# A list schedule that groups runs of quarter products and counts each change of tiling on TensorE

## The chip, the core and the metric

The kernel runs on one core of a Trainium2 chip. The metric is the device time of one execution in microseconds (us). TensorE is called PE here, VectorE DVE, ScalarE ACT, GpSimd POOL and the engine that issues the transfers SP, as in the profile.

## What is computed

Four layers follow each other on x of 128 graphs x 64 nodes x 256 features, all in fp32, with one 64 x 64 matrix adj for all graphs. Each layer is x = x + f(relu(layernorm(x))).

```python
# layer 0: two graph convolutions, then LSTMs over windows of p = 1..4 nodes
h = relu(adj @ (h @ Wg0 + bg0));  h = relu(adj @ (h @ Wg1 + bg1))
for p in 1, 2, 3, 4:
    wins = h[:, :nw * p].reshape(B * nw, p, D)          # nw = 64 // p
    h[:, p - 1 :: p] = lstm_last(Wih[p - 1], Whh[p - 1], bias, wins)
# layer 1: x' = L_norm @ x, a norm, attention of 4 heads masked by adj, an MLP, norms
# layer 2: attention from two vectors, softmax over adj, then (attention @ h) @ W
# layer 3: U^T h, two dense layers, then U (...): U the eigenvectors of a Laplacian of adj
```

L_norm needs the largest eigenvalue of adj, layer 3 all eigenvectors; the kernel works them out itself.

## The kernel before

Two graphs (128 tokens) make a tile. Eight tiles make one of eight groups of layer 0 (plan groups 0 to 7); layers 1 to 3 run on half-groups of four tiles (sixteen of them, plan groups REST = 10 to 25). `WEIGHTS` (8) and `ATTN` (9) are the loads and preparations of the later layers' weights, which take the place of the LSTM weights in SBUF; `EIG` (1000) is the eigenvector work, a long chain of small VectorE operations.

Nothing is issued in the order in which it is written. Each call is recorded as an `Op` of a `Plan`, with an engine, an assumed cost, and what it depends on. `Plan.schedule` then makes one order for each engine: a list schedule on an assumed clock `now[e]` of each engine. Among the operations that are ready on an engine it takes the one with the smallest rank, and `issue` writes the instructions in that order. The chip's engines run their own queues in that order, and wait on semaphores where the real times differ from the plan's. Two things limit what may be taken: `window`, how many groups ahead of the oldest unfinished one an operation may be, and the buffers (`big`, `mid`, `stat`, and eight PSUM `bank`s), of which some are kept in reserve for the oldest group.

The rank of an operation is its group (clamped), then the longest path of plan costs behind it; `EIG` goes first on PE and last elsewhere.

A *quarter product* is a product of 64 x 64 by 64 x 64 in one quarter of the PE array: multiplying by a block-diagonal matrix of two graphs (`mix`), or attention of one head (`layer1`). They are recorded in a `burst`: 32 of them (16 in the first group and in the second convolution of layer 3) are one operation of the plan, so they stay together in PE's queue. There are 132 bursts: 36 in layer 0 and 96 in layers 1 to 3 (six for each half-group). All other work on PE uses the full array of 128 rows. The plan charges a burst 0.1 + 0.034 us a product and knows nothing of what stands beside it.

Layer 0 (`layer0`) has a front (norms, two graph convolutions with their bursts, the products with Wg) and then the LSTM steps: for each of two halves of the hidden size the gates' products, sigmoid and tanh on ACT, and three VectorE operations. Every instruction is recorded through one helper, so all have one source line (L332) in the profile, and work is told apart by tiles: `adjTb` is the matrix of the convolutions of layer 0, `lapb`, `Ub` and `UTb` those of layers 1 and 3, `bank` any PSUM bank, `mids` the gates.

## Time and profile before

| | |
|---|---|
| time, median of 3 runs | 2208.51 us (2205.82 to 2208.59) |
| span of the profiled run | 2203.4 us, granted PE clock 0.998 |
| instructions | 42,023, of them 15,428 matmul records |
| quarter products on PE | 7,680 records of 64 x 64, each product two |
| DMA | 36.46 MB, 4.5% of the engines' time on the main queue |

Where the prediction speaks of the profile: the page gives busy time by engine and the chain of work that ended last; a table of stretches gives busy time of each engine between two times; the list of waits says for which engine and tile PE waited; and the timeline gives starts, merged over equal neighbours. Full fp32 products are two records as well, transposes one. Layer 0 fills the time up to about 1,390 us, with the first instruction of layer 1 on PE at about 1,247 us.

### The profile page before, as it was taken

What the parts mean: (1) busy time and instruction counts of PE and PEld (TensorE: products, weight loads), DVE (VectorE), ACT (ScalarE), POOL (GpSimd) and SP (SyncE); (2) the same over time, 40 slices, a digit from 0 to 9 for tenths busy, and PEclk for the clock granted to TensorE, in tenths of its full rate; (3) what the DMA queues carried; (4) which work ended last, traced back from release to release, by engine and by line L of the source; (5) the groups of instructions that cost most, each with busy time, mean ns of one, the idle gap of its engine ahead of it and who ended that gap; (6) DMA issues with size and microseconds to landing.
All of it is one profiled execution on the core that took longest, in us unless ns stands there. A gap on an engine that the chain in (4) does not pass through costs nothing.

```text
span 2203.4 us, 42023 instructions
## 1 busy us (share of the span) xinstructions
PE 2176.4 (99%) x15428; PEld 1494.9 (68%) x15428; DVE 1689.4 (77%) x7018; ACT 967.3 (44%) x1943; POOL 554.3 (25%) x856
## 2 busy tenths in 40 slices
PE   9999999999999999999999999999999999999998
PEld 6578468468558558558557657777767677776776
DVE  7678767769999999999885525468797678776697
ACT  4332443433323433423423533355466555455674
POOL 3101110200100100100100304145374546444353
PEclk9999999999999999999999999999999999999999
DMA  7000000010000000000000011000000000000001
GB/s 258 2 3 22 2 2 20 2 39 1 1 1 1 1 1 1 1 1 1 6 0 1 6 41 33 1 1 12 11 11 11 30 11 30 19 13 1 1 2 59
DMA packets 32255, 36.46 MB, mean 17 GB/s; under 512 B 8113, under 2 KB 29489, under 8 KB 31537
## 3 DMA queue, kind: packets, MB, share of 16 engines
q1 hardware_dynamic: 30944, 32.73, 4.5%
q8 instruction: 121, 1.98, 0.4%
q10 hardware_dynamic: 1104, 1.05, 0.2%
q14 instruction: 86, 0.70, 0.1%
HBM read 22.85 MB, written 10.49 MB: 15 GB/s over the span
## 4 chain that ended last, share of the span: by engine, by line
PE 86%; DVE 9%; POOL 2%; ACT 1%; issue 1%; DMA 0%; SPq 0%; DVEq 0%; ACTq 0%; POOLq 0%
PE bank L332 86%; DVE arena L332 3%; DVE stat L332 2%; DVE big L332 2%; DVE x L332 1%; POOL stat L332 1%; DVE mids L332 1%; ACT mids L332 0%; DVE Whh L332 0%; ACT arena L332 0%; ACT big L332 0%; POOL big L332 0%; POOL x L332 0%; ACT x L332 0%; DMA adj<-in_adj_dram 0%
## 5 line engine op out<-in xcount | busy, mean ns | idle before, releaser
L332 PE MATMUL bank<-big,Wih 128*128 128x512 f32 (+2 forms) x2312 | 772.5, 477 | 1.0 <-POOL big L332 0.5
L332 ACT ACTIVATE mids<-bank,bl 128x256 f32<-128x256 f32 (+2 forms) x624 | 343.5, 562 | 600.2 <-PE bank L332 587.0
L332 PEld LDWEIGHTS bank<-big,Wih 128*128 128x128 f32 x2312 | 430.4, 190 | 248.9 <-issue 153.1
L332 PE MATMUL bank<-big,Whh 128*128 128x256 f32 (+2 forms) x1608 | 495.1, 443 | 2.1 <-DVE big L332 2.1
L332 PEld LDWEIGHTS bank<-big,Whh 128*128 128x128 f32 x1608 | 302.7, 190 | 132.0 <-issue 60.3
L332 DVE TENSOR_TENSOR arena<-arena 64x21 f32<-64x21 f32 (+5 forms) x2255 | 360.1, 191 | 33.0 <-POOL arena L332 1.0
L332 POOL TENSOR_SCALAR stat<-stat 128x4 f32<-128x4 f32 (+1 forms) x228 | 62.2, 274 | 689.8 <-DVE stat L332 676.7
L332 DVE TENSOR_TENSOR big<-big,mids 128x256 f32<-128x256 f32 (+2 forms) x192 | 98.2, 511 | 138.3 <-ACT mids L332 136.9
L332 DVE TENSOR_TENSOR big<-mids 128x512 f32<-128x512 f32 (+2 forms) x246 | 136.4, 559 | 59.4 <-ACT mids L332 56.5
L332 PE MATMUL bank<-arena,Wih 128*128 128x512 f32 (+2 forms) x408 | 146.0, 500 | 0.9 <-DVE Wih L332 0.4
L332 ACT ACTIVATE mids<-big 128x256 f32<-128x256 f32 (+2 forms) x176 | 89.8, 510 | 103.8 <-DVE big L332 75.2
L332 DVE SCALAR_TENSOR_TENSOR arena<-arena 64x1 f32<-64x1 f32 (+15 forms) x567 | 116.2, 229 | 12.7 <-POOL arena L332 6.2
L332 POOL TENSOR_TENSOR stat<-stat,mhalf 128x4 f32<-128x4 f32 (+1 forms) x114 | 119.3, 1049 | 5.7
L332 PEld LDWEIGHTS bank<-arena,Wih 128*128 128x128 f32 x408 | 76.3, 190 | 51.4 <-issue 33.7
L332 DVE TENSOR_SCALAR arena<-arena 64x1 f32<-64x1 f32 (+9 forms) x537 | 102.1, 198 | 9.2 <-POOL arena L332 1.0
L332 ACT COPY mids<-bank 128x256 f32<-128x256 f32 (+1 forms) x132 | 57.0, 488 | 78.0 <-PE bank L332 73.7
L332 DVE BATCH_NORM_STATS2 stat<-x 128x6 f32<-128x256 f32 x232 | 84.8, 409 | 0.1
L332 POOL MEMSET arena<- 64x2 f32 (+5 forms) x72 | 7.9, 112 | 295.1 <-DVE arena L332 295.1
L332 POOL TENSOR_TENSOR arena<-arena 64x1 f32<-64x1 f32 x66 | 39.2, 594 | 166.0 <-DVE arena L332 102.2
L332 POOL TENSOR_TENSOR big<-big,B1T 128x512 f32<-128x512 f32 x28 | 30.9, 1111 | 187.0 <-DVE stat L332 169.7
L332 PE MATMUL bank<-Wih,big 128*128 128x256 f32 (+1 forms) x320 | 73.5, 366 | 0.9 <-DVE big L332 0.8
L332 PE MATMUL bank<-Wg,mids 128*128 128x256 f32 x256 | 64.6, 393 | 0.7 <-ACT mids L332 0.7
(351 smaller groups left out, 3361.5 us busy)
## 6 DMA issues: line engine op xcount, KB each, us to landing
x<-in_x_dram SPq DMA_DIRECT2D x7, 1024.0 KB, 14.1
out_dram<-x SPq DMA_DIRECT2D x24, 256.0 KB, 2.3
Wih<-in_WihT_dram SPq DMA_DIRECT2D x3, 1024.0 KB, 16.0
Whh<-in_WhhT_dram SPq DMA_DIRECT2D x3, 1024.0 KB, 12.0
put<-x SPq DMA_DIRECT2D x2, 1024.0 KB, 4.0
arena<-put SPq DMA_DIRECT2D x2, 1024.0 KB, 5.1
out_dram<-arena SPq DMA_DIRECT2D x8, 256.0 KB, 2.2
Whh<-in_W_dram SPq DMA_DIRECT2D x2, 512.0 KB, 3.9
```

The costliest lines, as they stand in the source:

```text
L332: getattr(self.engines[op.eng], name)(*map(real, args), **{k: real(a) for k, a in kw.items()})
```

## The change

The order of work changes, and nothing else: no instruction is added or removed. Three things do it.

- The plan now remembers whether PE last ran quarter products (`many`). Each change between these and full products costs 0.178 us on its clock, and a burst itself 0.029 us a product.
- A new term `back`, ahead of the group's rank, puts an operation of PE back. In a run of quarter products, full products stand back behind any burst that is ready. Outside one, a burst stands back unless two are ready or it has been ready for 20 us (layers 1 to 3; in layer 0 it doesn't stand back).
- The front of layer 0 has `lead` = 1: it ranks with the group in front of it, by its path, so it goes ahead of that group's LSTM. For layer 0 the path alone decides within a group, as it did.

```diff
         yield
-        self.run.cost = 0.1 + 0.034 * len(self.run.calls)
+        self.run.cost = 0.029 * len(self.run.calls)
         self.run.lat = self.run.cost + 0.22
+        self.run.many = True
...
+                runs = sum(op.many and op.ready <= now[e] for op in ops)
...
-                    rank = (t > now[e] + 1e-9, t if t > now[e] + 1e-9 else 0.0, self.rank(op))
+                    back = many and not op.many and e == "PE" or op.many and not many and runs < 2 and now[e] - op.ready < (0.0 if op.group < REST else 20.0)
+                    rank = (t > now[e] + 1e-9, t if t > now[e] + 1e-9 else 0.0, back, self.rank(op))
...
+            if e == "PE" and op.many != many:
+                many, cost, lat = op.many, cost + 0.178, lat + 0.178
...
-        g = min(max(op.group, 0), self.ends)
+        g = min(max(op.group - op.lead, 0), self.ends)
+        if op.group < REST:
+            return (g, 0, -op.path, op.index)
         return (g, 6 * max(op.group - g, 0) - op.path, op.index)
...
     def layer0(x):
+        plan.lead = 1
...
                 G.tensor_tensor(dst, dst, b1[1], op=ALU.add)
+        plan.lead = 0
         cs, hs = fm(), fm()
```

## The prediction

> **What bounds the kernel now.** First the page: share of each engine, then the chain that ended last.

> ```profile
> PE 2176.4 (99%) x15428; PEld 1494.9 (68%) x15428; DVE 1689.4 (77%) x7018; ACT 967.3 (44%) x1943; POOL 554.3 (25%) x856
> PE 86%; DVE 9%; POOL 2%; ACT 1%; issue 1%; DMA 0%; SPq 0%; DVEq 0%; ACTq 0%; POOLq 0%
> ```

> PE is busy 99% and carries 86% of the chain. A busy PE is not proof by itself, because the ends of matmuls are modelled[...]. So I go by starts. Next the busy time by stretch (us and instructions of PE, PEld, DVE, ACT, POOL, then clock, DMA share, GB/s): the start, layer 0, the change-over, layers 1 to 3, the tail.

> ```profile
> 0.00:100.00 100.00, 95.94 (x687) 59.61 (x688) 69.83 (x399) 37.10 (x90) 26.91 (x74) 0.97 0.42 143
> 100.00:1290.00 1190.00, 1187.22 (x5831) 781.93 (x5831) 965.61 (x4860) 440.68 (x985) 103.57 (x217) 1.00 0.02 6
> 1290.00:1390.00 100.00, 97.01 (x360) 67.77 (x359) 41.84 (x65) 34.17 (x69) 27.86 (x23) 1.00 0.13 37
> 1390.00:2150.00 760.00, 753.10 (x7776) 550.04 (x7774) 573.26 (x1580) 434.29 (x760) 375.20 (x513) 1.00 0.03 11
> 2150.00:2204.00 54.00, 43.10 (x779) 35.52 (x778) 38.88 (x118) 21.08 (x42) 20.77 (x29) 0.98 0.18 60
> ```

> PE idles 4.1, 2.8, 3.0, 6.9 and 10.9 us: 27.7 in all. No other engine is near its limit outside layer 0, where the eigenvectors' work fills the VectorE. So there are two things to win or lose: the PE's own work, and these idle stretches. What ends them, from the waits of PE for 100 to 1340 us (first two rows) and for 1340 to 2150 us (the rest); columns: total us, times, longest.

> ```profile
> PE bank L332 <- DVE mids L332: 1.4, 4, 0.4
> PE bank L332 <- POOL big L332: 0.5, 1, 0.5
> ...
> PE bank L332 <- DVE big L332: 2.1, 1, 2.1
> PE bank L332 <- ACT arena L332: 1.7, 3, 0.8
> PE bank L332 <- ACT x L332: 1.2, 1, 1.2
> ```

> Many small waits with different releasers, none systematic.

> **What a run of quarter products costs.** The timeline of PE (start, duration, count) shows one run of 64 records (one burst of 32 products; each product is two records[...]) and one of 128 (two bursts together):

> ```profile
> 1233.16 3.62 PE L332 MATMUL bank<-Wg,mids 128*128 128x256 f32 x16
> 1236.71 1.16 PE L332 MATMUL bank<-adjTb,mids 64*64 64x64 f32 x64
> 1237.80 0.70 PE L332 MATMUL bank<-Wg,mids 128*128 128x256 f32 x2
> ...
> 389.66 3.17 PE L332 MATMUL bank<-big,Wg 128*128 128x512 f32 x7
> 392.75 2.10 PE L332 MATMUL bank<-adjTb,mids 64*64 64x64 f32 x128
> 394.78 0.49 PE L332 MATMUL bank<-arena 128*128 128x128 f32 x2
> ```

> Full matmuls of 256 columns start 0.2157 us apart, of 512 columns 0.4293 us (medians of starts in the trace). 16 x 0.2157 = 3.45, so a next full matmul could have started at 1236.61; the run starts at 1236.71 and the next full matmul at 1237.80. The run took 1.19 us of PE, 0.10 of it before its first start. For 128 records: 389.66 + 7 x 0.4293 = 392.67, next 394.78, so 2.11 us. Two runs apart cost 2.38, together 2.11. Over all runs the medians are 1.185 us (64 records, 82 runs) and 2.119 us (128 records, 9 runs); a run of 192 took 3.052. That is a line: 0.0146 us a record, plus **0.25 us a run** (2 x 1.185 - 2.119 = 0.251).

> [...] going in costs 0.094 us beyond the full matmul's usual 0.216, coming out the rest.

> **The change part by part.**

> 1. *Adjacent runs (rank term `back`, `runs`, and 0.178 a change in the plan's clock).* Counting the changed program's PE instructions: 3,840 quarter products in both, but they stand in 83 runs instead of 113. Layer 0 goes from 31 to 30, layers 1 to 3 from 82 to 53; there single bursts fall from 71 to 21, pairs rise from 8 to 23, threes from 3 to 8, and one run has five. Saved: 30 x 0.251 = **7.5 us**. All but one of these merges lie before the last 100 us of PE work, where PE is busy over 99%, so each comes off the end unless a wait swallows it. If every wait after 1390 us (6.9 us) swallowed what it could of the savings, about 4 would be left: the low bound of this part; the high one is 7.5.

> 2. *The burst's price in the plan (0.029 a product instead of 0.1 + 0.034).* For 32 products 0.93 us plus two changes at 0.178 makes 1.28 for a lone run, against 1.19 measured (before: 1.19). No instruction changes; it acts through the order alone, so its time is in the other parts.

> 3. *Layer 0 up to the second graph convolution ranks with the group in front (`lead`).* Bursts and normalisations of group g+1 go before the LSTM of group g. It adds no instruction. It should remove the waits in which a burst came too soon after the operation that feeds it: four waits on "DVE mids", 1.4 us. In the new order I compared, for each PE instruction, the PE work standing between it and the PE instruction its operands come from with the durations of the ACT, VectorE and GpSimd operations in between (0.5 to 0.8 us each with the hand-over, an estimate from the rows of the page). Before, 7 places in layer 0 after the first 100 us don't fit; after, 4. In layers 1 to 3 up to the tail 6 become 2; in the tail 22 become 21. I book **-1.5 us** and keep -5 and +5 as ends.

> 4. *What it makes worse.* A lone burst of layers 1 to 3 is held up to 20 us until a second is ready. PE takes other ready work meanwhile, so it costs nothing while eight half-groups are in flight; what is queued behind the burst is only its own half-group's chain. And at the change-over three bursts (half-groups 10, 11, 12) now stand together in front of the last LSTM steps of group 7, where one stood before. The copies that empty the banks of two of them stand on ACT some 90 us of PE work later, because the SBUF tiles they write come free only when group 7 is done. Four of eight banks are held meanwhile, a fifth for the first half of it by a weight preparation, so the LSTM turns over on three and then four banks. A gate of 336 columns is 4 products x 2 x 0.282 = 2.26 us of PE, and its sigmoid on ACT 0.5, so three banks suffice in the steady state; at the step's edge fewer input products can be moved forward (about 3 x 1.1 = 3.4 us of them) to hide the sigmoid, the three VectorE operations, the tanh and the product (six operations, some 2.8 us when VectorE runs at 0.45 us each). That still hides it. It doesn't while GpSimd runs its fourteen additions to x (1.3 us each, some 20 us), when VectorE operations took 1.0 to 1.9 us in the trace: the 2.1 us wait on "DVE big" at 1380 us is that case. Bound: 0 to 8 us over the 3.0 that this stretch idles now; I take about 0 net, because the VectorE work of half-group 10, which shared this stretch before, moves behind it.

> 5. *Start and tail.* The first burst runs and the last sixteen stand nearly as before (15 or 16 runs in the last 100 us). 0, within 1.5 us.

> Sum: 2208.5 - 7.5 - 1.5 = **2199.5 us**.

> **The rivals.**

> *Waits shrink as well.* With bursts further from what feeds them, layer 0 loses its 2 us of waits and layers 1 to 3 half of 6.9: 2208.5 - 7.5 - 5.5 = 2195.5. For it: the count of places that don't fit. Against: most pauses there have a VectorE queue behind them, which the count doesn't see.

> [...] The LSTM of group 7 on three banks stalls some 0.5 us at each gate group of 5 step edges, and GpSimd's additions meet it: +5. With 7.5 saved: 2206, not to be told from no change. For it: the 2.1 us wait that is there already. Against: 2.26 us of PE a gate against 0.5 us of ACT.

> *Holding bursts starves the end (slower).* Each half-group has six bursts in its chain. If the holding makes the half-groups move in step, their VectorE and ACT phases bunch, and the idle time of layers 1 to 3 and of the tail doubles: 2208.5 - 7.5 + 6.9 + 10.9 = 2218.8. For it: VectorE is 75% busy there, and 53 runs of up to five bursts release work in lumps. Against: the tail's order is nearly unchanged.

> **How the numbers follow.** Main forecast 0.60, waits shrink 0.15, banks 0.13, starved 0.12. The bound for "faster" is 2208.5 x 0.998 = 2204.1; the first two fall under it: faster 0.75, same 0.13, slower 0.12. The range takes in the shrinking waits and the banks: 2191 to 2208.

> **What would show it.** Quarter-product runs: 83, each with 0.25 us beyond 0.0146 a record; PE's busy time down by some 7 us. Waits on "DVE mids" in layer 0 gone or down to one. Around 1290 to 1390 us, idle PE near 3 us if the banks suffice; waits on ACT or "DVE big" of over 6 us there would show the second rival. Idle over 10 us in 1390 to 2150, or over 15 in the tail, would show the third. [...]

## The result, and the profile after

The changed kernel takes **2199.16 us** (median of 4 runs, 2196.78 to 2199.61) against 2207.36 for the kernel before in the same comparison: ratio 0.9961, 95% interval 0.9944 to 0.9978. That is 8.2 us less, under half a per cent, and clear of the noise. The forecast was 2199.5. The first two rows of the page after answer to those of before: busy time by engine, and the chain that ended last.

```profile
PE 2164.7 (99%) x15428; PEld 1494.8 (68%) x15428; DVE 1691.9 (77%) x7018; ACT 958.0 (44%) x1937; POOL 569.8 (26%) x856
PE 93%; DVE 4%; POOL 1%; ACT 1%; issue 1%; DMA 0%; SPq 0%; DVEq 0%; ACTq 0%; POOLq 0%
```

The matmuls are the same 15,428, yet PE is busy 11.7 us less, and its share of the chain rises from 86% to 93%. The busy time by stretch:

```profile
0.00:100.00 100.00, 94.29 (x820) 61.10 (x821) 76.26 (x422) 34.46 (x85) 32.66 (x79) 0.98 0.42 143
100.00:1290.00 1190.00, 1189.47 (x5644) 781.35 (x5643) 959.43 (x4836) 438.50 (x987) 107.14 (x212) 1.00 0.02 6
1290.00:1390.00 100.00, 98.13 (x555) 70.72 (x554) 35.14 (x52) 34.17 (x69) 22.24 (x17) 1.00 0.13 34
1390.00:2150.00 760.00, 747.66 (x7821) 551.78 (x7820) 590.82 (x1620) 433.63 (x764) 392.62 (x525) 1.00 0.04 12
2150.00:2196.00 46.00, 35.15 (x594) 29.85 (x593) 30.27 (x90) 17.19 (x34) 15.19 (x23) 0.95 0.18 59
```

Idle PE is 5.7, 0.5, 1.9, 12.3 and 10.9 us. It fell in layer 0 (from 2.8) and at the change-over (from 3.0) and rose in layers 1 to 3 (from 6.9). In total it rose by 3.3 us, so by this view everything won is PE's own work. These idle figures lean on the ends of matmuls, which the profile models, and the 11.7 us with them: in the timeline below, the row from 1411.88 ends at 1414.91 by its duration and the next starts at 1414.73. So I also took the time from the first to the last matmul's start apart in three terms: every record at its usual distance to the next (2115.9 us in all kernels with this work), 0.251 us for each run of quarter products, and the rest (waits and stretches of slow clock):

| | first to last start | runs of quarter products | runs x 0.251 | rest |
|---|---|---|---|---|
| before | 2197.8 | 113 | 28.4 | 53.5 |
| after | 2189.4 | 83 | 20.8 | 52.6 |

30 runs fewer make 7.5 us, and the rest fell by 0.9. The rest is that of one profiled execution of each kernel, and differences of 2 or 3 us in it are not to be read: in the one of before the slow clock of the start lasts 6.8 us and in the one of after 3.4, with another 3.4 in the tail. A merged run looks like this in the timeline after, three bursts of 32 products as one row of 192 records:

```profile
1409.63 2.32 PE L343 MATMUL bank<-Wih,big 128*128 128x256 f32 x10
1411.88 3.03 PE L343 MATMUL bank<-lapb,arena 64*64 64x64 f32 x192
1414.73 0.74 PE L343 MATMUL bank<-lapb,big 64*64 64x64 f32 x35
1416.61 1.62 PE L343 MATMUL bank<-lapb,big 64*64 64x64 f32 x93 [1.13 <-issue]
1418.16 0.66 PE L343 MATMUL bank<-ident,big 128*128 128x128 f32 x4
```

From 1411.88 to 1414.73 is 2.85 us for 192 records, 0.0148 each; with one way in and out at 0.25 that is 3.10, where three lone runs would have taken 3 x 1.185 = 3.56. The same lines show the other side: this is the run of five bursts (320 records), and in it PE stands 1.13 us, put down to "issue", which means that the profile shows nothing that PE waited for.

Of layer 0's waits before (four on "DVE mids", one on "POOL big", one on "DVE big") one is left between 100 and 1340 us:

```profile
PE bank L343 <- DVE mids L343: 0.4, 1, 0.4
```

One thing did change beside the order: the loads of ACT's function tables depend on it, and there are 39 of them instead of 45, 1.28 us of ACT each in both traces (50.0 and 57.7 us in all). They are not the gain. ACT carries 1% of the chain in both kernels, and among the kernels below cost_only has 43 loads and is slower than before, and after_seven has 33 and is slower than after.

### The profile page after: what moved, and what is told of

Its sections match the earlier page's. It is cut to its first block, busy times and chain, and to the rows that moved or that the text cites. A ratio compares the mean times of both kernels' runs of the same rounds, so it can differ in the third digit from the quotient of the medians.

```text
span 2195.0 us, 41974 instructions
## 1 busy us (share of the span) xinstructions
PE 2164.7 (99%) x15428; PEld 1494.8 (68%) x15428; DVE 1691.9 (77%) x7018; ACT 958.0 (44%) x1937; POOL 569.8 (26%) x856
## 4 chain that ended last, share of the span: by engine, by line
PE 93%; DVE 4%; POOL 1%; ACT 1%; issue 1%; DMA 0%; SPq 0%; DVEq 0%; ACTq 0%; POOLq 0%
PE bank L343 93%; DVE stat L343 1%; DVE x L343 1%; POOL stat L343 1%; DVE big L343 1%; DVE arena L343 1%; DVE mids L343 1%; DVE Whh L343 0%; ACT mids L343 0%; ACT big L343 0%; POOL arena L343 0%; ACT x L343 0%; DMA adj<-in_adj_dram 0%; POOL Whh L343 0%; SPq L343 0%
## 5 line engine op out<-in xcount | busy, mean ns | idle before, releaser
L343 PE MATMUL bank<-big,Wih 128*128 128x256 f32 (+2 forms) x2576 | 854.4, 474 | 1.9 <-DVE big L343 1.4
L343 PEld LDWEIGHTS bank<-big,Wih 128*128 128x128 f32 x2576 | 481.0, 190 | 273.1 <-issue 163.5
L343 PE MATMUL bank<-big,Whh 128*128 128x256 f32 (+2 forms) x1640 | 506.9, 446 | 0.0
L343 PEld LDWEIGHTS bank<-big,Whh 128*128 128x128 f32 x1640 | 309.6, 190 | 142.1 <-issue 72.2
L343 POOL TENSOR_SCALAR stat<-stat 128x4 f32<-128x4 f32 (+1 forms) x228 | 69.0, 303 | 831.9 <-DVE stat L343 817.2
L343 DVE TENSOR_TENSOR big<-mids 128x512 f32<-128x512 f32 (+2 forms) x256 | 146.7, 578 | 64.2 <-ACT mids L343 60.1
L343 DVE SCALAR_TENSOR_TENSOR arena<-arena 64x1 f32<-64x1 f32 (+14 forms) x569 | 119.6, 233 | 16.4 <-POOL arena L343 11.2
L343 PE MATMUL bank<-Whh,big 128*128 128x256 f32 x336 | 83.8, 383 | 1.4 <-DVE x L343 0.7
L343 PEld LDWEIGHTS bank<-Whh,big 128*128 128x128 f32 x336 | 61.4, 190 | 19.3 <-issue 6.7
L343 ACT ACTIVATE arena<-arena 128x512 f32<-128x512 f32 (+28 forms) x70 | 20.8, 304 | 96.7 <-DVE arena L343 96.3
```

Of the source, the lines that this page charges most:

```text
L343: getattr(self.engines[op.eng], name)(*map(real, args), **{k: real(a) for k, a in kw.items()})
```

## The experiments

Each kernel ran beside the kernel before on the same chip. In the table, "rest" is the third term above, from the one profiled execution of each kernel (that of back_and_price took 2199.94 us, 4.3 less than its median; the others lie within 2.5 us of theirs); the three parts of the change are the term `back`, the prices on the plan's clock (0.029 a product, 0.178 a change) and the rank of layer 0 (`lead`).

| kernel | parts | time, us | ratio (95% interval) | runs | rest |
|---|---|---|---|---|---|
| before | none | 2207.1 to 2207.4 | 1 | 113 | 53.5 |
| lead_only | lead | 2206.85 | 1.0000 (0.9992 to 1.0009) | 109 | 54.7 |
| cost_only | prices | 2220.32 | 1.0063 (1.0051 to 1.0076) | 114 | 67.9 |
| back_only | back | 2210.77 | 1.0017 (1.0010 to 1.0023) | 77 | 67.9 |
| no_back | lead, prices | 2208.88 | 1.0005 (0.9997 to 1.0013) | 115 | 56.5 |
| back_and_price | back, prices | 2204.20 | 0.9986 (0.9979 to 0.9992) | 81 | 56.3 |
| back_and_lead | back, lead | 2241.32 | 1.0154 (1.0140 to 1.0168) | 82 | 98.8 |
| after | all | 2199.16 | 0.9961 (0.9944 to 0.9978) | 83 | 52.6 |

**One part alone.** First `back`:

```diff
-                    rank = (t > now[e] + 1e-9, t if t > now[e] + 1e-9 else 0.0, self.rank(op))
+                    back = many and not op.many and e == "PE" or op.many and not many and runs < 2 and now[e] - op.ready < (0.0 if op.group < REST else 20.0)
+                    rank = (t > now[e] + 1e-9, t if t > now[e] + 1e-9 else 0.0, back, self.rank(op))
```

> The kernel before plus the rank term `back` alone (burst price and rank of layer 0 as before, a change costs nothing on the plan's clock). Its PE order has 77 quarter-product runs instead of 113 (27 in layer 0, 50 after it). Theory 'each run costs 0.25 us of PE': 36 x 0.251 = 9.0 us less, waits within 3 us either way: 2195 to 2202 us against 2207.4 of before. Rival 'the earlier front of layer 0 and the better price do it': no more than 2 us less, 2205 to 2208.

Measured 2210.77. The runs came down to 77, worth 9.0 us, but the rest grew by 14.4. The expectation missed: it took the waits for nearly fixed, and they aren't.

`lead`, without `back` and the prices:

```diff
-        g = min(max(op.group, 0), self.ends)
+        g = min(max(op.group - op.lead, 0), self.ends)
+        if op.group < REST:
+            return (g, 0, -op.path, op.index)
```

> The kernel before plus the rank of layer 0 alone (lead = 1, rank by path). 109 runs instead of 113. Theory: 4 x 0.251 = 1.0 us less by the runs, and up to 2.4 us less by fewer waits in layer 0: 2203.5 to 2206.5. Rival 'the earlier front does it': 2198 to 2202.

Measured 2206.85, no change within some 2 us. The earlier front of layer 0 does not carry the result. Nor does it shorten the waits of layer 0 by itself: PE idles 2.9 us between 100 and 1290 us, as before (2.8).

The prices alone:

```diff
-        self.run.cost = 0.1 + 0.034 * len(self.run.calls)
+        self.run.cost = 0.029 * len(self.run.calls)
...
+            if e == "PE" and op.many != many:
+                many, cost, lat = op.many, cost + 0.178, lat + 0.178
```

> The kernel before plus the plan's prices alone (0.029 us a product and 0.178 a change on its clock), ranks as before. 114 runs instead of 113. Theory: no change within 3 us, 2204.5 to 2210.5. Rival 'a truer clock of the plan removes waits': 2198 to 2203.

Measured 2220.32, 13 us slower with one run more. The work is the same; the plan's clock moved by some tenths, its order with it, and the rest grew by 14.4. This missed too.

**All but one part.** The changed kernel with `back = False`:

> The changed kernel without the rank term `back` (prices and lead kept). 115 runs. Theory: it gives the whole saving of the runs back, 32 x 0.251 = 8.0 us over the 2199.2 of after, so 2207 within 3. Rival 'prices and lead do it': within 2 us of after, 2197 to 2201.

Measured 2208.88, as the theory of the runs had it: of the 9.7 us between it and after, 32 x 0.251 = 8.0 can be put down to the runs. The rival is out.

The changed kernel without the line `plan.lead = 1`:

> The changed kernel without the rank of layer 0 (lead = 0; `back` and the prices kept). 81 runs, so 32 x 0.251 = 8.0 us less than before by the runs. What the waits do is open: `back` alone and the prices alone each added some 14 us of waits. Theory A (the plan's clock overprices PE: 12.4 us too much with `back` alone, 11.3 with the prices alone, 7.8 here): waits near after's, 2197 to 2203. Theory B (the rank of layer 0 keeps the waits down): waits up 10 to 15 us, 2209 to 2215.

Measured 2204.20 (2199.94 to 2209.48), between the two theories and nearer to A. The profile shows a rest of 2.8 us over that of before, the medians (3.1 us less than before, with 8.0 saved by the runs) one of 4.9.

The changed kernel with the old price and no charge for a change:

```diff
-        self.run.cost = 0.029 * len(self.run.calls)
+        self.run.cost = 0.1 + 0.034 * len(self.run.calls)
...
-                many, cost, lat = op.many, cost + 0.178, lat + 0.178
+                many, cost, lat = op.many, cost, lat
```

> The changed kernel with the old price of a burst and no charge for a change on the plan's clock (`back` and the rank of layer 0 kept). 82 runs, so 31 x 0.251 = 7.8 us less than before by the runs. Theory A (the plan overprices PE by 11.1 us here): waits up 10 to 15 us, 2209 to 2215. Theory B (the rank of layer 0 keeps the waits down): waits within 3 us of before, 2197 to 2203.

Measured 2241.32. This refutes theory B and is far beyond theory A. The stretch shows where: busy time for 1390 to 1450 and 1450 to 1530 us, first back_and_lead, then after (columns as above).

```profile
1390.00:1450.00 60.00, 59.03 (x674) 46.27 (x674) 31.63 (x67) 23.78 (x48) 21.77 (x26) 1.00 0.01 2
1450.00:1530.00 80.00, 53.96 (x360) 34.70 (x359) 41.72 (x108) 27.68 (x47) 24.04 (x33) 0.79 0.00 1
```

```profile
1390.00:1450.00 60.00, 58.87 (x671) 45.27 (x670) 33.86 (x76) 26.60 (x54) 26.72 (x33) 1.00 0.01 2
1450.00:1530.00 80.00, 77.91 (x710) 56.14 (x712) 62.85 (x158) 38.22 (x67) 38.25 (x51) 1.00 0.01 1
```

Up to 1450 us the two are alike. Then back_and_lead gets 360 matmul records done on PE where after does 710. PE is busy for 54 of these 80 us, DVE for 42 and the others for less, so none of them is full. Its timeline of PE has one pause of 16.6 us:

```profile
1492.77 1.67 PE L343 MATMUL bank<-Whh,mids 128*128 128x256 f32 x7
1511.06 1.22 PE L343 MATMUL bank<-big,same 128*128 128x256 f32 x2 [16.62 <-DVE big L343]
```

What PE waits for is the one small product of layer 2 of half-group 10. DVE, POOL and ACT hand its norms and sums to each other meanwhile, one operation at a time, and this product is next in PE's order. That is a chain of one half-group running alone.

**Why only one half-group runs: theory A against theory C.** In the order of back_and_lead the half-groups 13 to 17 start together, as a run of five bursts, and into the bad stretch 14 to 17 still keep two tiles each of the pool `big`, 13 one or two: 15 to 18 of 20 are held, and the plan keeps six for the oldest half-group. The others then can't get their next tile (theory C). These counts are read from the plan's order. Against it stands theory A, that a wrong price on the plan's clock is the cause. One edit for each. The true price (0.125, which makes a lone run 1.18 us on the plan's clock), all else as in after:

> The changed kernel with 0.125 instead of 0.178 us a change on the plan's clock, which makes a lone run 1.18 us there, the measured price. 81 runs, 8.0 us less than before by the runs. Theory A (waits grow where the plan overprices PE; here by under 1 us): waits at or below after's, 2196 to 2201. Theory C (waits grow where the half-groups 13 to 17, started together, keep their tiles of the pool `big` so that only group 10 can go on; in this order 16 to 18 `big` tiles are held from 1393 to 1490 us of PE work and the half-groups 13 to 17 hold theirs, as in back_and_lead): 2212 to 2240, the waits between 1440 and 1530 us.

Measured 2240.62, ratio 1.0150 (1.0136 to 1.0164). Theory A falls as the whole cause: with the plan's clock at the measured price the kernel is as slow as back_and_lead, and by the same pause:

```profile
1484.78 4.05 PE L343 MATMUL bank<-Whh,big 128*128 128x256 f32 x18
1505.43 1.22 PE L343 MATMUL bank<-big,same 128*128 128x256 f32 x2 [16.60 <-DVE big L343]
```

And back_and_lead with seven half-groups in flight:

```diff
-        return max(oldest, 0) + 2 - oldest if oldest < NG - 1 else max(oldest, REST) + 8 - oldest
+        return max(oldest, 0) + 2 - oldest if oldest < NG - 1 else max(oldest, REST) + 7 - oldest
```

> back_and_lead (2241) with at most seven half-groups in flight instead of eight; prices as there. 83 runs. Theory C: fewer half-groups hold `big` tiles, the 17 us wait at 1511 us and the half clock after it are gone: 2197 to 2205. Theory A (the prices are the cause): still over 2225.

Measured 2206.77, ratio 0.9998 (0.9990 to 1.0006), with 83 runs and a rest of 62.7. The pause is gone, prices unchanged: 34.6 us for one half-group less in flight. That is what theory C expects, if 1.8 us over its range. It is one kernel, and a change of the number in flight changes the whole order; after has eight in flight too and no such pause. So the number in flight is shown to matter in this order, and the tiles of `big` as the cause are argued from the order alone.

Replaying the plan of back_and_lead adds two things. While half-group 10 runs alone, 12 and 13 want a tile of `big` and hold six of the eight PSUM banks, and 11 and 14 to 17 want a bank: two buffers are in it, and which of them should be larger stays open. And the pause stands in the plan itself, with PE idle for 17.3 us on the plan's clock in back_and_lead and in true_price, and for no more than 2.7 us at once in after. It could have been read there before a run. Small differences could not: on the plan's clock PE ends at 2178 us in lead_only and at 2180 in after, which measured 2207 and 2199.

**Two tries at a better version.** A lone burst of layer 0 held as well:

```diff
-                    back = ... and now[e] - op.ready < (0.0 if op.group < REST else 20.0)
+                    back = ... and now[e] - op.ready < (20.0 if op.group < REST else 20.0)
```

> The changed kernel with a lone burst of layer 0 held up to 20 us as well. 78 runs, 25 of them in layer 0 instead of 30; the order of layers 1 to 3 is that of after. 5 x 0.251 = 1.3 us less than after by the runs, and up to 1.5 us more of waits for bursts in layer 0: 2197 to 2200.5. A try at a better version.

Measured 2198.73 (2195.36 to 2199.66), ratio 0.9960 (0.9946 to 0.9973): not to be told from after. Five runs fewer are 1.3 us, and the rest grew by 1.9.

After with seven half-groups in flight:

> The changed kernel with at most seven half-groups in flight. 81 runs, 0.5 us less than after by the runs. Theory C: no starving in after, so nothing to win by it: 2197 to 2203. A second try at a better version.

Measured 2204.47, ratio 0.9986 (0.9980 to 0.9993). Two runs fewer, but a rest of 60.6, 8.0 more than after. In this order, where nothing starves, the eighth half-group in flight hides waits.

**The price of a run by itself.** A full-array product of one column goes into each burst of the kernel before, at its start or in its middle; the order of the operations is the same in both.

```diff
+    def mark(dst):
+        PE.matmul(dst, ones, ones[:, :1], start=True, stop=True)
...
+                    if c * nt + t == MARK * nc * nt // 2:
+                        mark(ps[0][:, nc * nt * N - 1:nc * nt * N])
```

> The kernel before with one more full-array product (128 rows, one column) at the start of each of the 132 bursts, in a place that the burst then overwrites. It breaks up the merged runs: 132 runs instead of 113. Control for the next kernel. 19 x 0.251 = 4.8 us by the runs, and 132 x 0.06 to 0.22 = 8 to 29 us by the products themselves: 2220 to 2242.

> The same product in the middle of each burst instead; the order of all operations is that of mark_first. 246 runs against 132. If a run costs 0.251 us of PE whatever stands in it: 114 x 0.251 = 28.6 us over mark_first, within 4. Rival 'the 0.25 us belongs to the first burst's operands or bank, not to the change of tiling': within 5 us of mark_first.

Measured 2227.49 and 2262.95: 35.5 us for 114 more runs, 0.31 a run. The rival is out, as the operands of a burst are the same in both, and the size is over the range that I gave. The timelines say why, first mark_mid, then mark_first:

```profile
899.00 1.89 PE L332 MATMUL bank<-big,Whh 128*128 128x256 f32 x8
900.82 0.69 PE L332 MATMUL bank<-adjTb,mids 64*64 64x64 f32 x32
901.45 0.38 PE L332 MATMUL bank<-ones 128*128 128x1 f32 x2
901.76 0.69 PE L332 MATMUL bank<-adjTb,mids 64*64 64x64 f32 x32
902.38 0.71 PE L332 MATMUL bank<-ident,big 128*128 128x128 f32 x4
```

```profile
895.59 1.89 PE L332 MATMUL bank<-big,Whh 128*128 128x256 f32 x8
897.32 0.28 PE L332 MATMUL bank<-ones 128*128 128x1 f32 x2
897.52 1.16 PE L332 MATMUL bank<-adjTb,mids 64*64 64x64 f32 x64
898.62 0.71 PE L332 MATMUL bank<-ident,big 128*128 128x128 f32 x4
```

Eight records of 256 columns end, by their usual distance, 1.73 us after they start, at 900.73 and 897.32. From there to the next full product it takes 1.65 us with the mark in the middle and 1.30 with the mark first: 0.35 for the split. In it the two records of the mark start 0.133 us apart inside a run and 0.029 after a full product (medians; after, which has ten products of this shape, shows 0.133 in the one that ends a run and 0.030 as the median of all), so I count 0.10 as the mark's own, and 0.25 is left for the run. That the 0.10 belongs to the mark and not to the change is argued; counted with the change, a split costs 0.35. My expectation had taken the mark's own time as the same in both places. (Over the whole kernel it is 0.31 a run and not 0.35, because PE idles 3.6 us less in mark_mid than in mark_first.)

## Why the prediction was right

**The runs** (-7.5): right in number and price. 83 runs stand in the trace, and the medians of the undisturbed runs keep to the line: 0.719 us for 32 records, 1.652 for 96, 2.118 for 128. Since the line holds over all these lengths, 0.25 us goes with a run and not with its records. Taking `back` away gives the gain back (no_back), and splitting bursts adds 0.25 to 0.35 us a run with the same operands (mark_mid). The runs give the price of a change and not what PE does in that time.

**The waits** (-1.5, ends -5 and +5): -0.9 in the profile, and that is luck. Two errors cancel. By starts the rest fell in layer 0 (7.8 to 4.4 us) and at the change-over (4.1 to 2.9), more than was booked; in layers 1 to 3 it rose (20.9 to 22.6), and so it did in the tail (9.5 to 11.1; the tail starts at 2150 us before and at 2142 after). The count of places that don't fit forecast the sign in layer 0, and a fall where the rise came. Nor does `lead` do it, to which the gain was booked: between 100 and 1290 us PE idles 0.5 us in after and in no_back, 2.9 with `lead` alone and 3.4 with `back` and the prices, so it took `lead` and the prices together. In the seven other orders with the term `back` that were run, the rest is 1 to 45 us over that of before, in five of them by 7 us or more.

The sum is closer than its working: it starts from 2208.5 us, and before measured 2207.4 in the comparison. The forecast was 9.0 us less, the result is 8.2.

**The banks at the change-over** (0 net): the second rival did not come. Waits on ACT and "DVE big" between 1290 and 1395 us are 1.9 us in all, where over 6 would have shown it; "DVE big" alone went from 2.1 us in one wait to 1.4 in two. (GpSimd's additions to x number sixteen in the trace before, not fourteen; the argument is the same.)

**Holding the bursts** (nothing, with 0.12 for a slower kernel): this step of the prediction was wrong, and the sum hides it. Idle PE in layers 1 to 3 is 12.3 us, over the 10 that I had named as the sign of the third rival (10.9 without a wait of 1.45 us shortly before 2144 us, which belongs to the tail). The kernel without `back` and otherwise the same, no_back, idles 7.7 us there:

```profile
1390.00:2150.00 760.00, 752.35 (x7816) 548.80 (x7818) 569.98 (x1587) 451.41 (x773) 380.80 (x518) 1.00 0.03 11
```

So the holding and grouping cost some 3 to 5 us there, in single profiles. That it is the third rival at a small size, half-groups in step, is argued. At full size the starving stands in back_and_lead and true_price, where it ends in one half-group running alone. I had looked for it in the tail, and it sits at the start of layer 1. My sentence that holding a burst costs nothing "while eight half-groups are in flight" had it backwards there: with seven in flight the pause is gone. In after the same run of five bursts stands in PE's queue, and by the plan's order it goes well because the half-groups 14 to 16 get their tiles and let go of them: they are down to one each by about 1460 us of PE work, while in back_and_lead and true_price they keep two.

**The price on the plan's clock** (its time booked in the other parts): it acts through the order alone, as predicted, but the prediction put no size on that, and the size is large. The change of prices alone cost 13 us (cost_only), where I expected none within 3; with `back` and `lead` in place, 0.178 against 0.125 is 2199 against 2241. The runs of the changed order were counted, and that part was sure. The waits were forecast from a count that the runs don't bear out, and it was luck that this order was not one of the bad ones.

## What to carry to other kernels

On a PE that is 99% busy, count the changes between full and quarter products in its queue: each run of quarter products cost 0.25 us beyond its records here, so putting two together is worth 0.25 us. When a list schedule makes the order, the saved PE time is sure and the waits are not: edits to the order alone changed the time by -0.4 to +1.5%, so judge the order that came out, stretch by stretch, look for long pauses on the plan's own clock first, and run the neighbours of a parameter before trusting it. Where no engine is full, look for a pool whose tiles are held by work that can't go on; one item less in flight was worth 35 us in one such order, and cost 5 us in one where nothing starved.

## What the runs showed of the hardware that was not expected

In the tail of after, short pauses cost more than their length. PE waits 1.46 and 1.22 us within 4 us of each other, and the clock granted is then 0.5 for 3.4 us (from 2157.5 us):

```profile
2155.41 1.16 PE L343 MATMUL bank<-arena,x 64*64 64x64 f32 x64 [1.46 <-ACT arena L343]
2157.79 3.50 PE L343 MATMUL bank<-Whh,Whh 128*128 128x256 f32 x8 [1.22 <-ACT Whh L343]
```

Eight such records take 1.89 us at full clock (before, from 2159.95 us), so this costs 1.6 us. The kernel before has nearly the same two waits there (1.43 and 1.16 us) and no slow clock. One wait of 2.1 us at the change-over is followed by 3.4 us at half clock in back_only and not in before. So in these runs the length of a pause alone doesn't decide it.

```profile
1378.70:1382.00 3.30, 1.22 (x6) 0.76 (x5) 3.06 (x5) 0.42 (x1) 1.97 (x2) 1.00 0.00 0
1382.10:1385.40 3.30, 3.30 (x9) 2.62 (x8) 0.28 (x1) 0.00 (x0) 0.00 (x0) 0.50 0.02 5
...
1375.80:1379.20 3.40, 2.19 (x11) 1.58 (x9) 3.40 (x3) 0.91 (x3) 3.17 (x3) 1.00 0.00 0
1379.20:1382.60 3.40, 2.50 (x12) 2.22 (x13) 1.23 (x4) 0.42 (x1) 0.00 (x0) 1.00 0.02 5
```

Why the clock falls there, the runs do not show.

In back_and_lead the long pause comes with 23.9 us at half clock (seven steps), from 1496.6 us (the mean clock from 1490 to 1510 us is 0.67); the two records after the pause then take 1.22 us, where such a pair takes 0.70 at full clock.
